# Neighbouring rows by transfers inside the chip, in place of a product with a banded matrix

## The chip, the cores and the metric

The kernel runs on one core of a Trainium2 chip. A core has a matrix engine (TensorE, PE in the profile; its weight loads are PEld), a vector engine (DVE), an activation engine (ACT), GpSimd (POOL) and SyncE (SP), which issues most of the transfers. Each engine works through its own queue of instructions in order; semaphores tie the queues together. Matrix products go from the on-chip buffer (SBUF, 128 partitions) into PSUM. Transfers run on the core's 16 DMA engines.

The metric is device time of one execution in microseconds (us). The median of several executions is given; a profiled execution beside them gives the trace.

## The reference

The input is 16 batches of 256 tokens by 256 features, all in fp32. Two layers follow each other, each with an attention and a feed-forward part:

```python
x = x + attn0(cross_attention(x, fside, ...), ...)
x = x + fp4_ffn(x @ W[cat] + b[cat], ...)
x = x + attn1(diffusion(x, zX, zY, zR), g_norm, W_qkv, W_out, pm)
x = x + mixture_of_experts(conditioned_mlp(x, ...), ...)
```

The change lies in `diffusion`, the step ahead of the second attention. `y` is the batch's x, with tokens as rows:

```python
yp_x = jnp.pad(y, ((0, 0), (0, 0), (1, 1)), mode='reflect')
lap_x = (yp_x[:, :, :-2] - 2.0 * y + yp_x[:, :, 2:]) / (dx * dx)
yp_y = jnp.pad(y, ((0, 0), (1, 1), (0, 0)), mode='reflect')
lap_y = (yp_y[:, :-2, :] - 2.0 * y + yp_y[:, 2:, :]) / (dy * dy)
du_dt = zX * lap_x + zY * lap_y + zR * y * (1.0 - y)
```

`lap_x` is the second difference along the features, `lap_y` the second difference along the tokens. At the edges the neighbour is reflected: token -1 is token 1, token 256 is token 254.

## The kernel before

The program has two parts. `woven` (L292) does everything up to the second attention for all 16 batches; `mixture` (L1034) does the conditioned MLP and the mixture of experts. The change is in the first.

A batch's x is one tile `x` of 128 partitions by 2 by 256 (token s x 128 + p lies in partition p, slot s), with five such buffers. Nine generators (the list in L310) describe the work: `stage_a` and `stage_e` the first attention, `stage_f` the first feed-forward, `stage_gate`, `stage_up` and `stage_down` the preparation of its weights, `stage_p`, `stage_g` and `stage_v` the second attention (projections, scores, values; four heads at a time, four steps n a batch). They hand single instructions to `weave` (L182), which decides while the program is built in which order each engine gets them. It keeps a planned time for each engine, each tile's last write and read (`written`, `read`), and a ring of buffers for each tag; the instruction that could start earliest goes next. Costs come from a table (L125), the hop from one engine to another is `HOP` (L126), and what SP issues counts as landed `LANDING` = 4.5 us after its issue (L127, L212). So the order of all engines is fixed in advance, from planned times; on the chip each engine then takes its instructions in this order and waits where a semaphore asks for it. `ready` (L191) computes the earliest start of an instruction: from the writes of its inputs and from the earlier writes and reads of its output's buffer.

`stage_p` (L798) loads constants once, among them the banded matrix `lap` (L801), then for each batch calls `diffuse` (L860) and four times `project4` (L897). Batch b is begun when the first feed-forward is done with it (`done["F"]`, L852), and step i = 4b + n when the values of step i - 3 have been issued (L855). `project4` loads `wq` (two buffers), `wv` (two) and `wo` (three) and multiplies them with `zT`; its last product is that of `wv`. `stage_f` issues two transfers of 1 MB of zeros to `ysort` after each batch (L612 to L614). All these loads and stores stand on SP's one queue.

`diffuse` takes a `single` PSUM bank and computes `ply` = `lap_y` there by four products with `lap` (L864 to L867; each is two records in the trace). POOL adds the left and right neighbours into `lx` (L869 to L871). Five DVE instructions make u (L872 to L876), the last of them adding zY x `ply` from PSUM. The bank is given back (L877), ACT squares u, and a few small instructions give the row's norm (L878 to L884). Four transposes on PE and two ACT copies make `zT`, tag `e_zT`, with one buffer (L885 to L892). The host builds the matrix in `tables` (L1438 to L1443).

Of the kernel before, what the change touches and what calls it, by code (L numbers as in the profile page):

```python
# [16 lines left out]
ALU = mybir.AluOpType  # L17
AX = mybir.AxisListType

P = 128  # L20
S = 256
D = 256
# [159 lines left out]
def weave(streams):  # L182

    free, written, read, rings = {}, {}, {}, {}
    turn = None
    names = lambda aps: [x.tensor.name for x in aps]

    def ready(op, engine):  # L191
        t = 0.0
        for n in names(op.ins):
            when, by = written.get(n, (0.0, engine))
            t = max(t, when + (HOP if by != engine else 0.0))
        for x in op.outs:
            n = x.tensor.name
            before = [written.get(n), read.get(n)]
            ring = rings.get(getattr(x.tensor, "tag", None), [])
            if n not in ring and ring:  # L200
                bufs = x.tensor.bufs or x.tensor.tag_meta.bufs
                if len(ring) >= bufs:
                    before += [written.get(ring[-bufs]), read.get(ring[-bufs])]
            for p in before:
                if p:
                    t = max(t, p[0] + (HOP if p[1] != engine else 0.0))
        return t

    def issue(op, choice, start):
        engine, cost, call = choice  # L210
        free[engine] = start + cost
        end = start + cost + (LANDING if engine == "SP" else 0.0)  # L212
        for n in names(op.ins):
            if end > read.get(n, (0.0, engine))[0]:
                read[n] = (end, engine)
        for x in op.outs:
            n, tag = x.tensor.name, getattr(x.tensor, "tag", None)
            written[n] = (end, engine)
            if tag is not None and n not in rings.setdefault(tag, []):
                rings[tag].append(n)  # L220
        call()

    def least(want):

        return min(want.free, key=lambda x: ready(Op([], [x], []), "PE"))


    waiting = [[s, None, None] for s in streams]
    while waiting:
        best, moved = None, False  # L230
        for rank, w in enumerate(waiting):
            while w[1] is None or (callable(w[1]) and w[1]()):
                moved = True
                try:
                    w[1], w[2] = w[0].send(w[2]), None
                except StopIteration:
                    w[0] = None
                    break
            if w[0] is None or callable(w[1]):
                continue  # L240
            if isinstance(w[1], Want):
                if not w[1].free:
                    continue
                op = Op([("PE", 0.0, None)], [least(w[1])], w[1].ins)
            else:
                op = w[1]
            for c in op.choices:
                start = max(ready(op, c[0]), free.get(c[0], 0.0))
                if c[0] == "PE" and w is not turn:
                    start += TURN  # L250
                key = (start, rank, c[1])
                if best is None or key < best[0]:
                    best = (key, w, c, start)
        waiting = [w for w in waiting if w[0] is not None]
        if best is not None:
            _, w, c, start = best
            if isinstance(w[1], Want):
                w[2] = least(w[1])
                w[1].free.remove(w[2])
            else:  # L260
                issue(w[1], c, start)
                if c[0] == "PE":
                    turn = w
            w[1] = None
        else:
            assert moved, "all streams wait"
# [12 lines left out]
def mm_(g, out, pairs, start=True, stop=True):  # L279

    last = len(pairs) - 1
    for i, (lhsT, rhs) in enumerate(pairs):
        yield g.pe.matmul(out, lhsT, rhs, start=start and i == 0, stop=stop and i == last)


def copy_(g, dst, src):

    a, v = g.act.copy(dst, src), g.dve.tensor_copy(dst, src)
    return Op(a.choices + v.choices, a.outs, a.ins)
# [23 lines left out]
def load(g, pool, name, shape, src):  # L313

    t = pool.tile(shape, F32, name=name)
    return t, g.sp.dma_start(out=t, in_=src)
# [12 lines left out]
def single(g, *ins):  # L329

    return (yield Want(g.singles, ins))
# [167 lines left out]
def row32(j, n):  # L499
    return slice(32 * j, 32 * j + n)  # L500
# [293 lines left out]
def tile_l(g, shape, name, bufs=1, tag=None):  # L794
    return g.l_.tile(shape, F32, name=name, tag=tag or name, bufs=bufs)


def stage_p(g):  # L798
    k, a = g.k, g.a
    yield lambda: g.done["A"] > 0 and g.done["W"] == 3  # L800
    g.lap, op = load(g, g.w, "lap", [P, 2, S], a["lap"])  # L801
    yield op
    g.z = []
    for n in ("condB_zX", "condB_zY", "condB_zR"):
        t, op = load(g, g.w, n, [P, g.B], a[n].unsqueeze(0).to_broadcast([P, g.B]))
        g.z.append(t)
        yield op
    g.gn, op = load(g, g.w, "g", [P, 2], a["g"])
    yield op
    g.cos1, op = load(g, g.w, "cos1", [P, S], a["cos1"])  # L810
    yield op
    g.sin1, op = load(g, g.w, "sin1", [P, S], a["sin1"])
    yield op

    g.pmo = g.w.tile([P, 2, D], F32, name="pmo")
    pmv = tile_l(g, [P, 2, 2, 2 * P], "wq", 2)
    yield g.sp.dma_start(out=pmv, in_=a["pmv"].rearrange("p c (r w) -> p c r w", r=2))
    for c in range(2):
        wo = tile_l(g, [P, 4, D], "wq", 2)
        yield g.sp.dma_start(out=wo, in_=a["w_out1"][:, 4 * c : 4 * c + 4, :])  # L820
        pmvT = tile_l(g, [P, 4, P], "f_pT", 3)
        one = yield from single(g, pmv)
        pt = one.rearrange("p (i t) -> p i t", i=4)
        for i in range(4):
            yield g.pe.transpose(pt[:, i, :], pmv[:, c, i // 2, (i % 2) * P : (i % 2 + 1) * P], g.ident)
        yield copy_(g, pmvT, pt)
        g.singles.append(one)
        one = yield from single(g, pmvT, wo)
        pm = one[:, :D]
        yield from mm_(g, pm, [(pmvT[:, i, :], wo[:, i, :]) for i in range(4)])  # L830
        yield copy_(g, g.pmo[:, c, :], pm)
        g.singles.append(one)

    g.cosq, g.sinq = g.w.tile([P, S], F32, name="cosq"), g.w.tile([P, S], F32, name="sinq")
    yield g.pool.tensor_scalar(g.cosq, g.cos1, DH1**-0.5, None, ALU.mult)
    yield g.pool.tensor_scalar(g.sinq, g.sin1, DH1**-0.5, None, ALU.mult)


    g.keys = []
    for n in range(4):  # L840
        pmk = tile_l(g, [P, 2, 4 * PM], "pmk", 2)
        yield g.sp.dma_start(out=pmk, in_=a["pmk"][:, n])
        t = g.w.tile([P, 2, 2, PM + P], F32, name=f"keys{n}")
        for j in range(4):
            rows = row32(j, 32)
            src = pmk[rows, :, j * PM : (j + 1) * PM]
            yield g.pool.tensor_copy(t[rows, :, :, 0:PM], src.unsqueeze(2).to_broadcast([32, 2, 2, PM]))
        g.keys.append(t)
    g.mhalf = g.w.tile([P, 2], F32, name="mhalf")
    yield g.pool.memset(g.mhalf, -0.5)  # L850
    for b in range(g.B):
        yield lambda b=b: g.done["F"] > b  # L852
        zT = yield from diffuse(g, b)
        for n in range(4):
            yield lambda i=4 * b + n: i < g.done["V"] + 3  # L855
            g.live[4 * b + n] = yield from project4(g, n, zT)
            g.done["P"] += 1


def diffuse(g, b):  # L860

    zx, zy, zr = (z[:, b : b + 1] for z in g.z)
    y = g.x[b]
    one = yield from single(g, y)  # L864
    ply = one.rearrange("p (s d) -> p s d", s=2)
    for st in range(2):
        yield from mm_(g, ply[:, st, :], [(g.lap[:, c, st * P : (st + 1) * P], y[:, c, :]) for c in range(2)])  # L867
    lx, u = tile_l(g, [P, 2, D], "e_lx"), tile_l(g, [P, 2, D], "e_u")
    yield g.pool.tensor_tensor(lx[:, :, 1 : D - 1], y[:, :, 0 : D - 2], y[:, :, 2:D], ALU.add)  # L869
    yield g.pool.tensor_tensor(lx[:, :, 0:1], y[:, :, 1:2], y[:, :, 1:2], ALU.add)  # L870
# [2 lines left out]
    yield g.dve.scalar_tensor_tensor(u, y, zr, u, ALU.mult, ALU.mult)  # L873
    yield g.dve.scalar_tensor_tensor(lx, y, -2.0, lx, ALU.mult, ALU.add)
    yield g.dve.scalar_tensor_tensor(u, lx, zx, u, ALU.mult, ALU.add)
    yield g.dve.scalar_tensor_tensor(u, ply, zy, u, ALU.mult, ALU.add)  # L876
    g.singles.append(one)  # L877
    ms = tile_l(g, [P, 2], "e_ms", 2)  # L878
    for st in range(2):
        yield g.act.activation(lx[:, st, :], u[:, st, :], AF.Square, accum_out=ms[:, st : st + 1])  # L880
# [5 lines left out]
    one = yield from single(g, u)  # L886
# [623 lines left out]
```

## Time and profile before

| | |
|---|---|
| time, median of 3 runs | 2941.87 us (2941.02 to 2943.33) |
| the profiled execution | 2943.53 us |
| its span, first instruction to last | 2941.8 us |
| mean granted clock of TensorE | 0.963 |
| woven part, to PE's last product before `xs` | about 1896 us |
| transfers | 265.66 MB, mean 90 GB/s |

What PE waited for longest between 200 and 1780 us of the span (total us, times, longest):

| waited for | us | times | longest |
|---|---|---|---|
| POOL `d_h` | 16.8 | 12 | 2.5 |
| POOL `c_y` | 11.0 | 9 | 3.7 |
| ACT `f_oT` | 7.4 | 15 | 0.7 |
| ACT `f_pT` | 6.5 | 15 | 1.5 |
| POOL `f_prob` | 6.4 | 3 | 4.6 |

Names are those of the program's tiles, without their numbers; `f_q<-f_t,f_t` is an instruction that writes `f_q` and reads two tiles `f_t`. Shapes are partitions by elements. Nearly all instructions of the woven part bear the line L160, as `Unit` makes them there; they are told apart by their tiles. The profile's busy time of PE sums records that overlap, so PE's price for a group of matmuls is read from the starts of the group and of the next one.

### The profile page before, as it was taken

How to read it: one execution, taken by the hardware profiler on the slowest of the kernel's cores; microseconds unless marked ns; L12 is line 12 of the kernel's file. 1: busy time of each engine (PE TensorE's matmuls, PEld its weight loads, DVE VectorE, ACT ScalarE, POOL GpSimd, SP SyncE). 2: the span in 40 equal slices, each digit the busy share in tenths (PEclk: the TensorE clock that was granted, in tenths of full speed). 3: DMA queues.
4: the chain of work that ended last, by engine and by line, in shares of the span. 5: the costliest groups of instructions: out<-in, count | busy, mean ns of one | idle time of the engine just before them, and what ended most of it. 6: DMA issues, size and time to landing. Idle time of an engine off the chain costs nothing. (4 is left out here: it accounts for less than half of the span.)

```text
span 2941.8 us, 42036 instructions
## 1 busy us (share of the span) xinstructions
PE 2768.7 (94%) x15979; PEld 2072.5 (70%) x15979; DVE 1428.6 (49%) x3073; ACT 924.0 (31%) x2416; POOL 842.2 (29%) x1023
## 2 busy tenths in 40 slices
PE   5899999999999999999999989689999999999999
PEld 3666667777777777767777767545566888888865
DVE  6566666676676676675776655413240000000023
ACT  2223333333333333423334333223321222222221
POOL 4333333433344343343343333202220000000034
PEclk7799999999899999999999999889999999999999
DMA  3122122122122132222221222231111355555523
GB/s 107 55 93 73 53 92 84 56 80 74 59 91 69 58 97 69 63 92 69 64 92 35 76 90 74 87 93 51 51 38 67 108 179 179 179 181 179 177 85 95
DMA packets 191230, 265.66 MB, mean 90 GB/s; under 512 B 34217, under 2 KB 161970, under 8 KB 181682
## 3 DMA queue, kind: packets, MB, share of 16 engines
q1 hardware_dynamic: 184882, 246.16, 26.2%
q0 software_dynamic: 6144, 16.79, 1.8%
q8 instruction: 128, 2.10, 0.3%
q14 instruction: 76, 0.62, 0.1%
HBM read 202.34 MB, written 60.56 MB: 89 GB/s over the span
## 5 line engine op out<-in xcount | busy, mean ns | idle before, releaser
L160 ACT ACTIVATE f_prob<-pair,f_stat 128x144 f32<-128x144 f32 x512 | 190.7, 377 | 270.2 <-DVE f_stat L160 258.8
L160 DVE TENSOR_TENSOR pair<-pair,mask 128x256 f32<-128x256 f32 (+1 forms) x384 | 197.8, 516 | 123.1 <-PE pair L160 83.2
L49 PE MATMUL bank<-ysT,w 128*128 128x256 f32 x1120 | 249.3, 381 | 5.7 <-ACT ysT L113 5.7
L160 PE MATMUL single<-e_zT,wq 128*128 128x256 f32 x1024 | 254.1, 392 | 0.0
L1155 POOL DMA_INDIRECT got<-osort,pos_o x64 | 62.3, 973 | 662.8 <-ACT hT L1103 608.5
L49 PE MATMUL bank<-w,ehT 128*128 128x256 f32 x1120 | 247.4, 379 | 0.0
L49 PEld LDWEIGHTS bank<-ysT,w 128*128 128x128 f32 x1120 | 211.3, 190 | 38.0 <-ACT ysT L113 9.9
L49 PEld LDWEIGHTS bank<-w,ehT 128*128 128x128 f32 x1120 | 212.8, 190 | 28.9
L160 PEld LDWEIGHTS single<-e_zT,wq 128*128 128x128 f32 x1024 | 193.4, 196 | 32.9 <-issue 2.7
L1140 ACT ACTIVATE ehT<-bank,own_b 128x256 f32<-128x256 f32 x280 | 132.5, 473 | 241.6 <-PE bank L49 241.6
L160 POOL TENSOR_SCALAR_AFFINE_SELECT b_e<-b_e 128x512 f32<-128x512 f32 x128 | 86.5, 676 | 329.9 <-ACT b_e L160 329.9
L160 PE MATMUL pair<-keys,f_q 32*128 32x144 f32 x2048 | 164.9, 300 | 0.9 <-ACT b_e L160 0.7
L160 PEld LDWEIGHTS pair<-keys,f_q 32*128 32x128 f32 x2048 | 137.2, 190 | 35.9 <-issue 28.6
L160 ACT ACTIVATE b_e<-pair 128x768 f32<-128x768 f32 x128 | 103.6, 810 | 166.4 <-PE pair L160 153.3
L160 PE MATMUL single<-wo,f_oT 128*128 128x256 f32 x512 | 129.8, 386 | 9.5 <-ACT f_oT L160 8.4
L160 POOL TENSOR_TENSOR f_q<-f_t,f_t 128x256 f32<-128x256 f32 x128 | 91.6, 734 | 160.9 <-DVE f_t L160 151.4
L160 PE MATMUL pair<-b_qkT 16*128 16x128 f32 (+1 forms) x1024 | 127.3, 373 | 11.0 <-ACT b_qkT L160 8.0
L1145 DVE COPY eo<-bank 128x512 f32<-128x512 f32 x35 | 24.2, 692 | 230.9 <-PE bank L49 230.9
L160 DVE TENSOR_REDUCE qpad<-pair 128x2 f32<-128x256 f32 (+1 forms) x256 | 131.0, 554 | 4.4
L1259 POOL DMA_INDIRECT ysort<-r_y,r_posi x64 | 62.6, 978 | 241.0 <-DMA ysort<-r_y,r_posi 97.0
L160 DVE TENSOR_TENSOR x<-x,single 128x512 f32<-128x512 f32 (+1 forms) x112 | 68.0, 607 | 128.7 <-PE single L160 128.1
L160 POOL TENSOR_TENSOR keys<-f_t,f_t 128x256 f32<-128x256 f32 x128 | 95.2, 762 | 118.8 <-DVE f_t L160 117.6
(295 smaller groups left out, 5319.7 us busy)
## 6 DMA issues: line engine op xcount, KB each, us to landing
w<-in_w SPq DMA_DIRECT2D x70, 1024.0 KB
ysort<-zero SPq DMA_DIRECT2D x32, 1024.0 KB
wq<-in_w_qk SPq DMA_DIRECT2D x128, 256.0 KB
wv<-in_w_v SPq DMA_DIRECT2D x64, 256.0 KB
wo<-in_w_out SPq DMA_DIRECT2D x64, 256.0 KB
ys<-ysort SPq DMA_DIRECT2D x35, 256.0 KB
osort<-eo SPq DMA_DIRECT2D x35, 256.0 KB
xT<-in_xT SPq DMA_DIRECT2D x16, 256.0 KB
```

Of the source, the lines that this page charges most:

```text
L49: nc.tensor.matmul(out, lhsT, rhs, start=start and i == 0, stop=stop and i == last)
L160: return Op([(self.name, self.cost(fn, outs, aps), lambda: call(*args, **kw))], outs, aps)
L1140: nc.scalar.activation(hT[:, f, :], ph, AF.Gelu_apprx_tanh, bias=b1[:, f : f + 1])
L1145: nc.vector.tensor_copy(o, po)
L1155: nc.gpsimd.indirect_dma_start(out=g, out_offset=None, in_=k.osort[:, :], in_offset=bass.IndirectOffsetOnAxis(ap=r.pos_o[:, i, t : t + 1], ...
L1259: nc.gpsimd.indirect_dma_start(out=k.ysort[:, :], out_offset=bass.IndirectOffsetOnAxis(ap=posi[:, i, t : t + 1], axis=0), in_=y, in_offset ...
```

## The change

The banded matrix and its four products go. In their place six transfers from SBUF to SBUF bring the neighbouring rows: `up` gets the row of token t - 1 and `down` that of token t + 1, each as one transfer of 127 partitions, one row of 256 from the other slot, and one reflected row. `up` is a tile of its own (tag `e_up`, one buffer), `down` uses the tag `e_zT`, whose one buffer holds `zT` later in the batch. POOL adds `down` to `up`, DVE subtracts 2y, and the last DVE instruction takes this tile where it took the PSUM bank. In `ready`, an earlier write or read of the output's buffer by SP no longer delays another instruction of SP.

```diff
@@ -202,7 +202,7 @@
                 if len(ring) >= bufs:
                     before += [written.get(ring[-bufs]), read.get(ring[-bufs])]
             for p in before:
-                if p:
+                if p and not p[1] == engine == "SP":
                     t = max(t, p[0] + (HOP if p[1] != engine else 0.0))
         return t
 
@@ -798,8 +798,6 @@
 def stage_p(g):
     k, a = g.k, g.a
     yield lambda: g.done["A"] > 0 and g.done["W"] == 3
-    g.lap, op = load(g, g.w, "lap", [P, 2, S], a["lap"])
-    yield op
     g.z = []
     for n in ("condB_zX", "condB_zY", "condB_zR"):
         t, op = load(g, g.w, n, [P, g.B], a[n].unsqueeze(0).to_broadcast([P, g.B]))
@@ -861,10 +859,17 @@
 
     zx, zy, zr = (z[:, b : b + 1] for z in g.z)
     y = g.x[b]
-    one = yield from single(g, y)
-    ply = one.rearrange("p (s d) -> p s d", s=2)
-    for st in range(2):
-        yield from mm_(g, ply[:, st, :], [(g.lap[:, c, st * P : (st + 1) * P], y[:, c, :]) for c in range(2)])
+
+    up, down = tile_l(g, [P, 2, D], "e_up"), tile_l(g, [P, 2, D], "e_zT")
+    for dst, src in (
+        (up[1:P], y[0 : P - 1]),
+        (down[0 : P - 1], y[1:P]),
+        (up[0:1, 1, :], y[P - 1 : P, 0, :]),
+        (down[P - 1 : P, 0, :], y[0:1, 1, :]),
+        (up[0:1, 0, :], y[1:2, 0, :]),
+        (down[P - 1 : P, 1, :], y[P - 2 : P - 1, 1, :]),
+    ):
+        yield g.sp.dma_start(out=dst, in_=src)
     lx, u = tile_l(g, [P, 2, D], "e_lx"), tile_l(g, [P, 2, D], "e_u")
     yield g.pool.tensor_tensor(lx[:, :, 1 : D - 1], y[:, :, 0 : D - 2], y[:, :, 2:D], ALU.add)
     yield g.pool.tensor_tensor(lx[:, :, 0:1], y[:, :, 1:2], y[:, :, 1:2], ALU.add)
@@ -873,8 +878,9 @@
     yield g.dve.scalar_tensor_tensor(u, y, zr, u, ALU.mult, ALU.mult)
     yield g.dve.scalar_tensor_tensor(lx, y, -2.0, lx, ALU.mult, ALU.add)
     yield g.dve.scalar_tensor_tensor(u, lx, zx, u, ALU.mult, ALU.add)
-    yield g.dve.scalar_tensor_tensor(u, ply, zy, u, ALU.mult, ALU.add)
-    g.singles.append(one)
+    yield g.pool.tensor_tensor(up, up, down, ALU.add)
+    yield g.dve.scalar_tensor_tensor(up, y, -2.0, up, ALU.mult, ALU.add)
+    yield g.dve.scalar_tensor_tensor(u, up, zy, u, ALU.mult, ALU.add)
     ms = tile_l(g, [P, 2], "e_ms", 2)
     for st in range(2):
         yield g.act.activation(lx[:, st, :], u[:, st, :], AF.Square, accum_out=ms[:, st : st + 1])
```

## The prediction

> **What bounds the kernel now.** I read the page's busy shares and clock first, then the busy time by stretch, then who TensorE (PE) waits for, then the instructions that the change touches.
>
> ```profile
> PE 2768.7 (94%) x15979; PEld 2072.5 (70%) x15979; DVE 1428.6 (49%) x3073; ACT 924.0 (31%) x2416; POOL 842.2 (29%) x1023
> ...
> PEclk7799999999899999999999999889999999999999
> ...
> q1 hardware_dynamic: 184882, 246.16, 26.2%
> ```
>
> PE is the full engine and its clock is nearly whole; the transfers that SP issues (q1) fill a quarter of sixteen engines. By stretch (start:end, length, then PE, PEld, DVE, ACT, POOL busy with counts, clock, DMA share, GB/s):
>
> ```profile
> 400.00:800.00 400.00, 384.08 (x2674) 290.64 (x2674) 275.43 (x554) 143.57 (x424) 151.34 (x185) 0.96 0.23 73
> 800.00:1200.00 400.00, 382.65 (x2617) 290.32 (x2614) 277.91 (x556) 143.37 (x430) 156.23 (x183) 0.98 0.25 79
> 1800.00:2000.00 200.00, 163.67 (x885) 115.26 (x884) 73.56 (x186) 56.99 (x162) 43.49 (x64) 0.90 0.29 84
> ```
>
> In the woven part (to about 1896 us) PE is 96% busy: a microsecond taken from PE is a microsecond won, and a microsecond in which PE is held up is lost, as no idle time is there to catch up in. What the change touches:
>
> ```profile
> L160 PE MATMUL single<-x,lap x128: 379/379/483, 174.0 to 1817.9; 128*128 128x256 f32 x128
> L160 POOL TENSOR_TENSOR e_lx<-x x48: 189/290/1662, 174.3 to 1816.2; 128x2 f32<-128x2 f32 x32, 128x508 f32<-128x508 f32 x16
> L160 DVE SCALAR_TENSOR_TENSOR e_lx<-x,e_lx x16: 680/684/1115, 176.4 to 1819.0; 128x512 f32<-128x512 f32 x16
> L160 DVE SCALAR_TENSOR_TENSOR e_u<-single,condB_zY,e_u x16: 750/751/752, 177.9 to 1820.5; 128x512 f32<-128x512 f32 x16
> ```
>
> Matmul records overlap, so their price is read from starts in order of time (start, length):
>
> ```profile
> 1816.41 1.89 PE L160 MATMUL single<-x,lap 128*128 128x256 f32 x8
> 1818.14 1.03 PE L160 MATMUL single<-wo,f_oT 128*128 128x256 f32 x4
> ...
> 1865.53 1.10 PE L160 MATMUL single<-ident,f_prob 128*128 128x128 f32 x8
> ...
> 1868.29 1.09 PE L160 MATMUL single<-f_pT,f_v 128*64 128x128 f32 x16
> ...
> 1881.29 1.99 PE L160 MATMUL single<-wo,f_oT 128*128 128x256 f32 x8
> 1888.34 1.97 PE L160 MATMUL single<-ident,f_prob 128*128 128x128 f32 x8 [5.05 <-POOL f_prob L160]
> 1890.23 2.18 PE L160 MATMUL single<-f_pT,f_v 128*64 128x128 f32 x16
> ```
>
> One banded product holds PE from 1816.41 to 1818.14, 1.73 us. And after a gap of 5.05 us the same two groups take 1.97 and 2.18 us where they took 1.10 and 1.09: a gap costs 2.0 us more than its length.
>
> [...] No transfer of the kernel before has 127 rows[...]: of the nine-row load `b2` (L1053) one record stands at 1913.24 us, at its issue, and nine follow at 1917.15 to 1917.57, while the 128-row `wo` issued at 1833.01 shows sixteen (1835.00 to 1836.51). [...]
>
> **The change part by part.** *Removed:* the product, 16 x 1.73 = 27.7 us of PE time on the bounding engine; the table's load (256 KB, once); one `single` bank a batch. All 27.7 us count as gain.
>
> *Added on POOL and DVE:* a 128x512 add on POOL (0.73 to 1.06 us by the other 256 and 512 wide rows) and one more `scalar_tensor_tensor` on DVE (0.68 us); the last one reads SBUF where it read PSUM (0.75, unchanged). POOL is 29% and DVE 69% busy in this part: nothing for the work itself. What counts is what these instructions wait for.
>
> *Added on SP:* six transfers a batch. SP issues one in 0.33 to 0.6 us, so about 2.6 us; SP mostly waits itself (1344 us in all for PE to release `single` tags), so the issue is free. Their duration is not. The trace's packets of 2048 bytes take 84 ns at the median, so 127 of them on one engine take 10.7 us; from the q1 line, 26.2% x 16 x 2941.8 us for 246.16 MB, the mean rate over all sizes makes it 13.0 us. Spread over sixteen it would be 0.7 us, and the landing that of `wo`, 2 to 3.5 us from issue. I take one engine and 10.7 us for each of the two big ones, in series; 13.0 and the sixteen-way spread are the ends.
>
> *When each starts.* `down` takes the buffer tag `e_zT`, so its transfer waits until PE has read the last `zT` of the batch before (the `wv` product of its fourth `project4`). `up` has a buffer of its own, and stands on SP right behind the `wo` load of that `project4`, so it starts earlier. By the order of PE's instructions in the changed program, with the prices of the trace (0.216 us a 256-wide record, 0.109 a transpose, 1.18 a group of sixteen `keys` records), `up` has 21.4 us of PE work ahead of `down` in batches 4, 6, 8, 10, 12: it is hidden. In 3, 5, 7, 9, 11 it has 14.7 us, and two 1 MB writes of zeros to `ysort` stand just ahead of it, which take about 8 us to land in the trace (issued 305.48, landed 313.6 to 315.3): `up` ends at 1 + 8 + 10.7 = 19.7, and `down` begins 4 to 5 us late.
>
> *What waits.* From that last read: 0.2 to issue, 1.0 to the first packet (as `wo` shows), 10.7, about 1.2 to the semaphore and through the four small transfers behind it: 13.1 us. Then POOL's add, 1.1, and hand-over: DVE continues at 14.6. Both engines work in order. The plan in the program puts POOL's add where a landing of 4.5 us allows it, so behind it on POOL wait the `affine_select` of `b_e` and the `keys`/`q` sums, and behind the waiting DVE instruction the mask additions, `f_stat` reductions and PSUM copies that PE needs next. In batch 4, PE's first such instruction (`a_eT`, `f`) stands 10.6 us of PE work after the last read, and DVE's copy for it comes 3.9 us after DVE continues, 18.5: a stall of about 8. In batch 5 the first is `pmo`,`f_ppT` after 6.6 us, and its copy is done at 17.3, with the 4 us lateness 21.2: a stall of 14.6. Batches 4 to 12 even: 5 x 8.1 = 40.5; 3 to 11 odd: 5 x 14.6 = 73. Batch 0 has both transfers in series from the moment x is final (0.4 + 1 + 21.4 + 0.8, add and chain 5, less 9.7 of PE work): 18. Batches 1, 2, 13, 14, 15, by the same count with 16.2, 8.6, 11.2, 8.8 and 5.8 us of work up to the `e_u` transposes: 9, 11, 10, 13, 15. Together 189.5 us.
>
> Clock after each stall: 2.0 us after 5 us idle is shown; I take 1.5 on average, 24 us. Waits that PE has already at these places and that the stall swallows: about 0.5 us a batch of the 5 us that PE idles in each, 8 us.
>
> *The planner's edit* (an SP transfer no longer counts the landing of an earlier SP transfer on the same tile) closes up the pairs of loads at the start and reorders everything. PE idles 46 us of the first 200; I bound the effect by -15 and +15 us and take 0.
>
> Sum: 189.5 + 24 - 27.7 - 8 = +178 us on the profiled execution's 2943.5 (its span is 2941.8 and 1.7 lies around it): 3121.5. The median of the runs is 2941.9, so 3120.
>
> **The rivals.** *Spread transfers, faster:* if the 127 rows go over sixteen engines, all six land within some 6 us of the trigger, the chain to `e_u` ends at about 11.5 us against 9.8 to 13.3 us of PE work, and stalls of 0 to 1 us a batch leave -27.7 + 8: 2922, at best 2914. This decides if a big transfer lands in under about 7 us. For it speaks that no trace here shows 127 rows; against it the nine-row load. Chance 0.10.
>
> *Half covered:* one engine, but PE, once free, has work that the stall has only displaced, or `up` and `down` run faster from SBUF than HBM loads did: 5 us a batch, 80 + 16 - 28 = +68, 3010. PE's 4% idle speaks against it. Chance 0.15.
>
> *Nothing covered:* 13 us each and both on the path in every batch, with the weight loads behind them on that engine late too: 26 + 3 + 5 - 11 = 23 us a batch, 368 + 32 - 28, some 3315. SP's order (`up` early) speaks against it. Chance 0.11.
>
> **How the numbers follow.** The forecast's case has 0.62, 3120, by itself 3050 to 3200; the rivals 0.10, 0.15, 0.11; 0.02 is left to a change of under 0.2% (5.9 us, about what a measurement of this kernel tells from no change), where spread transfers meet a worse order. The range 2985 to 3270 holds the forecast, the half-covered case and the near part of the last; outside lie the faster case and about 0.07 above. Faster 0.10, same 0.02, slower 0.88.
>
> **What would show it.** PE's busy time falls by about 31 us of records (128 fewer), and its waits grow. In the waits, POOL's `e_up` sum waits on a transfer, 5 to 20 us sixteen times; the clock dips below 0.9 in the woven slices; the mixture from the first `xs` transposes on lasts as long as before. If `e_up`'s add waits under 2 us, the transfers were spread and I am wrong about the sign; if it waits long and PE does not, the cover is bigger than I counted.

## The result, and the profile after

| | before | after |
|---|---|---|
| median of the runs, us | 2941.5 | 3125.0 |
| span of the profiled execution, us | 2941.8 | 3121.6 |
| ratio to before | | 1.0629 (95% interval 1.0608 to 1.0651) |
| mean granted clock of TensorE | 0.963 | 0.926 |

The forecast was 3120. The page of the changed kernel, in the lines that answer to those shown of before:

```profile
PE 2808.8 (90%) x15851; PEld 2097.8 (67%) x15851; DVE 1450.5 (46%) x3121; ACT 903.1 (29%) x2384; POOL 857.9 (27%) x1039
...
PEclk7889998899899899899998988869999999999999
...
q1 hardware_dynamic: 190882, 254.29, 25.4%
```

PE has 128 matmuls fewer and is still busy longer, at a lower clock: many of the 9s of before are 8s now over the first two thirds. The queue q1 moves 8 MB more, for a slightly smaller share of the time. By stretch (start:end, length, then PE, PEld, DVE, ACT, POOL busy with counts, clock, DMA share, GB/s), in the changed kernel:

```profile
400.00:800.00 400.00, 362.45 (x2370) 272.16 (x2368) 258.58 (x523) 124.86 (x377) 142.62 (x171) 0.92 0.23 74
800.00:1200.00 400.00, 358.48 (x2357) 270.84 (x2358) 250.10 (x503) 126.68 (x374) 142.59 (x173) 0.89 0.23 73
```

PE lost both busy share (96% to 90%) and clock (from 0.97 to about 0.9). The same view over the whole woven part and over what follows it, first of the kernel before:

```profile
0.00:1896.00 1896.00, 1759.88 (x11772) 1324.73 (x11772) 1250.03 (x2505) 659.98 (x1941) 715.88 (x879) 0.95 0.23 73
1896.00:2941.00 1045.00, 1008.78 (x4208) 747.82 (x4207) 178.55 (x568) 264.04 (x475) 126.36 (x144) 0.98 0.38 121
```

and of the changed one:

```profile
0.00:2075.60 2075.60, 1800.45 (x11644) 1350.15 (x11644) 1272.18 (x2553) 638.72 (x1909) 731.02 (x895) 0.90 0.22 71
2075.60:3121.00 1045.40, 1008.30 (x4207) 747.67 (x4207) 178.30 (x568) 264.35 (x475) 126.83 (x144) 0.98 0.38 121
```

The mixture is unchanged (1045 us, PE busy 1008). All of the loss is in the woven part, 179.6 us longer: PE is busy 40.6 us longer (1800.45 - 1759.88) and idle 139 us longer (275.2 against 136.1).

Where PE is idle begins at POOL. The instructions on the tile `e_up` (duration min/median/max in ns, then what the engine waited for ahead of them, us and times):

```profile
L160 SPq DMA_DIRECT2D e_up<-x x48: 579/772/9897, 175.9 to 1977.5; - x48
...
L160 DVE SCALAR_TENSOR_TENSOR e_up<-x,e_up x16: 692/1098/1100, 202.0 to 1988.5; 128x512 f32<-128x512 f32 x16
...
  DMA e_zT<-x: 176.7, 16
  POOL e_up L160: 129.6, 16
```

All sixteen sums wait for a transfer, 11 us on average, and DVE then waits for the sum. In order of time, batch 5 (start, length, what the engine was idle for ahead of it):

```profile
817.71 0.66 SPq L160 DMA_DIRECT2D e_zT<-x  x1
818.42 4.37 SPq L160 DMA_DIRECT2D e_up<-x  x1
...
832.33 1.26 POOL L160 TENSOR_TENSOR e_up<-e_up,e_zT 128x512 f32<-128x512 f32 x1 [13.58 <-DMA e_zT<-x]
833.63 1.10 DVE L160 SCALAR_TENSOR_TENSOR e_up<-x,e_up 128x512 f32<-128x512 f32 x1 [11.04 <-POOL e_up L160]
...
836.74 1.22 PE L160 MATMUL single<-pmo,f_ppT 128*128 128x256 f32 x2 [11.32 <-DVE f_ppT L160]
837.75 1.91 PE L160 MATMUL single<-wo,f_oT 128*128 128x256 f32 x4
```

`down` (`e_zT<-x`) is issued at 817.71, the sum begins 14.6 us later, DVE goes on, and its copy for PE comes last: PE stands 11.32 us. The `wo` group that then follows takes 1.91 us where it took 1.03. How long PE stays slow is seen in short stretches of the same view (clock third from the end):

```profile
837.00:840.00 3.00, 3.00 (x8) 2.25 (x8) 0.62 (x2) 0.24 (x2) 0.56 (x1) 0.50 0.00 0
...
849.00:852.00 3.00, 3.00 (x8) 2.37 (x8) 1.21 (x4) 0.00 (x0) 0.00 (x0) 0.50 0.00 0
852.00:855.00 3.00, 3.00 (x16) 2.22 (x16) 1.49 (x3) 0.28 (x1) 1.41 (x2) 0.85 0.00 0
```

Half speed from 837 to past 852: some 16 us of work done at half rate, 8 us lost beside the 11.32. This batch is the dearest of its kind. The 15 us from the end of the stall, in batches 5, 7 and 9, and from the end of a gap of only 1.90 us in batch 6:

```profile
836.70:851.70 15.00, 14.96 (x64) 10.57 (x65) 5.40 (x13) 2.56 (x8) 3.81 (x4) 0.50 0.22 70
1084.70:1099.70 15.00, 15.00 (x99) 11.15 (x101) 8.49 (x19) 4.00 (x13) 5.86 (x7) 0.88 0.23 72
1327.00:1342.00 15.00, 15.00 (x98) 11.15 (x100) 8.48 (x20) 4.03 (x13) 5.86 (x7) 0.88 0.22 70
949.30:964.30 15.00, 13.83 (x43) 9.90 (x44) 10.81 (x21) 3.72 (x14) 4.08 (x4) 0.57 0.63 203
```

The stalls of batches 3, 7, 9 and 11 are as long as that of batch 5 and cost about 2 us of clock each. The short gap of batch 6 costs 6 us.

### The profile page after: what moved, and what is told of

It is laid out like the page before. It is cut to its first block, busy times and chain, and to the rows that moved or that the text cites. A ratio compares the mean times of both kernels' runs of the same rounds, so it can differ in the third digit from the quotient of the medians.

```text
span 3121.6 us, 42067 instructions
## 1 busy us (share of the span) xinstructions
PE 2808.8 (90%) x15851; PEld 2097.8 (67%) x15851; DVE 1450.5 (46%) x3121; ACT 903.1 (29%) x2384; POOL 857.9 (27%) x1039
## 5 line engine op out<-in xcount | busy, mean ns | idle before, releaser
L160 PE MATMUL single<-wo,f_oT 128*128 128x256 f32 x512 | 142.9, 416 | 21.2 <-ACT f_oT L160 15.3
L160 PE MATMUL pair<-b_qS,b_qkT 17*128 17x256 f32 (+1 forms) x1024 | 127.0, 369 | 16.4 <-DVE qpad L160 10.0
L160 PEld LDWEIGHTS pair<-b_qS,b_qkT 17*128 17x128 f32 x1024 | 100.5, 204 | 51.9 <-issue 23.9
L160 PEld LDWEIGHTS single<-wo,f_oT 128*128 128x128 f32 x512 | 101.5, 208 | 43.9 <-ACT f_oT L160 18.8
```

Source lines behind the costliest of these rows:

```text
L160: return Op([(self.name, self.cost(fn, outs, aps), lambda: call(*args, **kw))], outs, aps)
```

## The experiments

Each ratio is to the kernel before on the same chip. The first four kernels ask what of the change makes the loss.

**The long transfers cut in two.** The 127 rows go as 112 and 15, which is called spread below:

```diff
-        (up[1:P], y[0 : P - 1]),
-        (down[0 : P - 1], y[1:P]),
+        (up[16:P], y[15 : P - 1]),
+        (down[0:112], y[1:113]),
+        (up[1:16], y[0:15]),
+        (down[112 : P - 1], y[113:P]),
```

> Each of the two 127-row transfers is cut into one of 112 rows and one of 15 rows; all else as in the changed kernel. Theory one-engine (a transfer of 127 rows runs on one DMA engine, two of 10.7 us each, and POOL's sum waits for the second): the pieces [...]land about 3.5 us after issue, POOL's sum waits under 2 us a batch (11 in the changed kernel), and the time falls to 2915 to 2940, near 2922. Rival order (the new order of instructions and the planner's edit cost the time, whatever the transfers do): 3080 to 3125. Rival any-wait (any transfer on the path stalls the queues): sum's wait stays over 5 us, time over 3030.

Measured: 2978.7 us, ratio 1.0117 (1.0102 to 1.0133). The waits ahead of the sum, in this kernel's `e_up` view:

```profile
  DMA e_zT<-x: 53.0, 10
  POOL e_up L160: 21.3, 7
```

Of the 183 us 146 are gone, with nothing altered in the source but the number of rows; PE takes its matmuls in the same order as in the changed kernel at 95% of the places. But none of the three ranges holds: the time lies 39 us above the first, and the sum waits 3.3 us a batch where under 2 were expected. On how many engines the pieces ran is not shown. The product's time is gone as well, and the kernel is still slower than before.

**The same, cut into 122 and 5 rows:**

> As e1, but cut into 122 rows and 5 rows[...]. Theory one-engine: the big parts take 61 x 84 ns = 5.1 us each in place of 10.7, down lands 5.5 us earlier, POOL's sum waits about 8 us in the odd batches and nothing in the even ones; between e1 and the changed kernel, 2990 to 3050. Rival order: 3080 to 3125, as in e1.

Measured: 3014.8 us, 1.0245 (1.0229 to 1.0260). Cut here, 110 of the 183 us are gone. This lies in the expected range, which took the row of packets to be half as long, 61; that is not shown. What is shown is the wait of POOL's sums for transfers: 87.3 us in all, about half of the 176.7 of the changed kernel, and 56.3 with 112 and 15 rows. That more than half of the loss goes with half of the wait would fit a landing of which a part stays covered. The three kernels together show that the loss follows this wait: 183, 73 and 37 us.

**The planner's edit alone**, on the kernel before:

```diff
-                if p:
+                if p and not p[1] == engine == "SP":
```

> The kernel before with the planner's edit in ready alone; the product with the banded matrix stays. Theory one-engine: the edit costs or gains at most 15 us, 2927 to 2957. Rival order: most of the +183 us is here, 3050 to 3125.

Measured: 2937.4 us, 0.9986 (0.9979 to 0.9992). By itself it is worth 4 us.

**The change without that edit:**

> The changed kernel without the planner's edit in ready. The three transfers into each tile then count as landing one after the other, 3 x 4.5 = 13.5 us, near the 14.4 us measured from down's issue to POOL's sum, so the plan puts other work there. Theory one-engine with a plan that counts too little: POOL's sum waits under 3 us a batch, PE's stalls go, 2920 to 2970. If the transfers hurt in another way (weight loads behind them on that engine, queue of SP blocked), the time stays over 3030.

Measured: 2978.0 us, 1.0124 (1.0107 to 1.0141). With the transfers the edit is not small at all: it costs 147 us. Without it the plan counts the three transfers into each tile one after the other, 3 x 4.5 us, and puts the sum later; with it the plan believes in 4.5 us. The time lies 8 us above the expected range, and POOL still waits (104.7 us in all, against 176.7; under 3 us a batch were expected, and most waits are of 7). PE is idle 189 us in the woven part, against 275, and works in another order. Spreading and planning each cure most of the loss, and both leave some 36 us. The next kernels look for these.

**A buffer of its own for `down`.** Two small scratch tiles are shared to make room (those lines are left out here):

```diff
-    up, down = tile_l(g, [P, 2, D], "e_up"), tile_l(g, [P, 2, D], "e_zT")
+    up, down = tile_l(g, [P, 2, D], "e_up"), tile_l(g, [P, 2, D], "e_down")
```

> The changed kernel, but `down` has a buffer of its own instead of taking turns with zT in e_zT (room for it: two of the four small scratch tiles of the down and up weights' quantization are shared). All six transfers can then be issued with `up`, 17 to 22 us ahead of the sum, and still go to one DMA engine in their long parts. If the loss is the wait between the release of e_zT and the landing: most of the 183 us goes, 2905 to 2965 us, and the sum on GpSimd waits under 40 us in all instead of 177. If the one engine's time itself were the loss (two transfers of 10.7 us in one row, 22 us), waits of 2 to 8 us in the odd batches stay and the time is 2980 to 3040. If the loss were the added elementwise work or the plan's order, 3090 to 3125.

Measured: 3068.1 us, 1.0426 (1.0380 to 1.0471). None of the three ranges holds. The second has the cause, two transfers in one row, but too small a wait. What SP issues in batch 5 of this kernel (start, length):

```profile
794.24 1.43 SPq L160 DMA_DIRECT2D e_up<-x  x1
796.11 7.91 SPq L160 DMA_DIRECT2D e_down<-x  x1
804.08 10.26 SPq L160 DMA_DIRECT2D e_up<-x  x1
814.39 1.27 SPq L160 DMA_DIRECT2D e_down<-x  x1
...
816.97 1.31 SPq L160 DMA_DIRECT2D wq<-in_w_qk  x2
```

and what the DMA engines move from 790 to 826 us, in 40 slices of 0.9 us, with the mean busy share of the sixteen in tenths:

```profile
DMA  0001799999971000000000000010000398600000
GB/s 0 0 0 27 225 312 370 372 360 364 353 246 36 14 27 25 25 25 34 25 25 23 25 25 25 25 41 26 25 27 25 94 302 285 228 23 23 23 19 6
```

After the zeros for `ysort` (370 GB/s) the rate sits at 25 GB/s from 802 to 818, about what one packet of 2048 bytes every 80 ns makes (25.6; the 80 ns are from the changed kernel), and the busy share is under a tenth in all but one of these slices (one engine of sixteen is 0.06): both long transfers on one and the same engine, one after the other. The sum begins at 824.6, 30.4 us after `up` was issued, more than the 17 to 22 us won. In batch 5 of the changed kernel the two were issued 18 us apart (800.01 and 817.71), and `up` had landed by 818.53. The buffer moves `down` from behind `zT` to behind `up`. In the even batches from 2 to 12 the sum no longer waits; in batches 5, 7, 9 and 11 it waits 11.6 to 11.8 us, and in 13 and 14 over 15.

**The same without the planner's edit:**

> The own buffer with the planner's line as it was before (a transfer waits in the plan for the landing of the one before it into the same tile). The plan then puts the sum six landings later, and the real landing lies well ahead of it. If the landing is all that counts: 2900 to 2945 us, at or below the own buffer with the edit. If a later sum costs by itself (the chain of diffuse starts the next batch's work later): 2955 to 2985, as without the edit before.

Measured: 3076.9 us, 1.0449 (1.0411 to 1.0486): neither expectation. The plan counts some 13.5 us where 25 to 31 are needed; the sum of batch 14 waits 19.2 us. All sums together wait less than with the edit (89.1 us against 134.4), and the time is no shorter; why was not found.

**Own buffer and spread transfers together:**

> The own buffer for `down` together with the 112 and 15 rows. If what stayed of the loss with spread transfers (about 36 us above the kernel before, though the product's 27.7 us are gone) is the 6.5 us from the issue of `down` to the sum: 2900 to 2935 us, faster than the kernel before. If it is the two operations more in the chain (sum on GpSimd 1.26 us, one more pass on VectorE 0.7 to 1.1 us, 16 batches) or the clock of another order: 2965 to 2985, as with spread transfers alone.

Measured: 2961.9 us, 1.0071 (1.0050 to 1.0091), with this left in the `e_up` view:

```profile
  DMA e_down<-x: 5.7, 1
```

This lies 3 us below the second expectation. PE takes its matmuls in exactly the order of the kernel with the own buffer alone, so the 106 us between these two are the spreading and nothing else. From 750 to 786 us of this kernel no stretch at 25 GB/s is left, and the one-row transfers land 2.6 (`up`) and 1.7 us (`down`) after their issue, where those of `up` took 19.7 in the stretch above. Now the transfers are hidden, one sum in sixteen waits, and the kernel is still slower than the one with the product. So landing explains at most 17 of the remaining 36 us and not the rest.

**No second difference along the tokens at all:**

> Leaves out the second difference along the tokens altogether: no product, no transfers, no sum, no two passes on VectorE. The floor for every version. If the product's 16 x 1.73 us of TensorE lie on the path: 2890 to 2918 us. If the clock or the order takes part of it back: 2918 to 2945.

Measured: 2880.5 us, 0.9783 (0.9745 to 0.9820), below both expectations. The kernel before is 62 us slower, and 57 us when the planner's edit, which this kernel has, is counted there too (2937.4). That is the price of the product, of the DVE pass that reads it and of the order of instructions that goes with them, where 28 us were counted.

**The added work without the transfers, and the transfers without the work:**

```diff
-    yield g.pool.tensor_tensor(up, up, down, ALU.add)
+    yield g.pool.tensor_tensor(up, y, y, ALU.add)
```

> Neither product nor transfers: the sum on GpSimd adds y to itself, and the two passes on VectorE follow as in the changed kernel, so the output leaves the neighbouring rows out. With an own buffer and spread transfers the sum waits only 5.7 us in all, yet 81 us stand between that kernel (2962) and the one without any of it (2880.5). If these are the price of the sum (16 x 1.3 us on GpSimd), of the passes (32 x 0.7 to 1.1 us on VectorE) and of the order they make: 2940 to 2970 us. If they are the price of the eight transfers (SP's issues, the queue): 2880 to 2900 us.

> The eight transfers into two own buffers, and nothing that reads them: no sum, no passes, no product, so the output leaves the second difference along the tokens out. If the elementwise work is the price: 2880 to 2900 us. If the transfers are: 2940 to 2965 us. In between, 2900 to 2940: each has a part of it.

Measured: 2964.0 us, 1.0077 (1.0051 to 1.0103), for the work alone; 2881.2 us, 0.9803 (0.9776 to 0.9829), for the transfers alone. Eight transfers a batch, spread and early, cost nothing measurable (2881.2 against 2880.5). This is a clean comparison: PE takes its matmuls in the same order in both kernels, the same tiles at 99.9% of 15851 places. The kernel with the work alone has the time of the own and spread version (2961.9), and its order too, again at 99.9% of the places. Between the two pairs lie 83 us. But between them the order changes as well: only 46% of the places agree. So 83 us is the price of the sum and its two passes together with the order that `weave` makes for them; no run keeps the order. Their own engine time is about 45 us (16 x 1.3 on POOL, 32 x 0.75 on DVE). The woven part, first without any of it, then with the work alone:

```profile
0.00:1837.00 1837.00, 1703.95 (x11644) 1291.81 (x11644) 1268.12 (x2506) 648.23 (x1924) 729.69 (x879) 0.95 0.24 76
0.00:1919.30 1919.30, 1766.27 (x11644) 1328.75 (x11644) 1282.67 (x2548) 641.81 (x1914) 734.77 (x895) 0.93 0.23 72
```

With the same 11644 matmuls PE is idle 20 us longer and busy 62 us longer. The clock records have it at half speed for 250 us of its busy time, against 158: this makes 46 of the 62 us, and 16 stay open. By stretch, first without any of it, then with the work alone:

```profile
400.00:800.00 400.00, 383.34 (x2740) 294.16 (x2738) 290.98 (x572) 148.85 (x452) 163.96 (x192) 0.97 0.23 73
800.00:1200.00 400.00, 383.85 (x2761) 293.80 (x2761) 298.32 (x584) 149.24 (x446) 166.64 (x194) 0.98 0.25 79
```

```profile
400.00:800.00 400.00, 376.22 (x2534) 284.83 (x2533) 276.31 (x546) 136.41 (x414) 152.74 (x181) 0.94 0.23 73
800.00:1200.00 400.00, 379.12 (x2547) 287.41 (x2547) 271.33 (x547) 134.17 (x407) 154.80 (x184) 0.95 0.23 72
```

PE's busy share falls only by 1 to 2%, and its matmul count by 8%. What happens is seen in the latter kernel at 522 to 530 us, PE's rows:

```profile
522.93 0.92 PE L160 MATMUL pair<-b_qkT 16*128 16x128 f32 x8
525.86 0.92 PE L160 MATMUL pair<-b_qS,b_qkT 17*128 17x256 f32 x8 [2.00 <-DVE qpad L160]
526.71 3.41 PE L160 MATMUL single<-e_zT,wq 128*128 128x256 f32 x8
```

and the DVE rows that end in this wait:

```profile
522.53 0.52 DVE L160 TENSOR_SCALAR q_big<-q_big 128x704 int32<-128x704 int32 x1
523.15 0.89 DVE L160 SCALAR_TENSOR_TENSOR q_y<-q_big,q_xn 128x704 f32<-128x704 f32 x1
523.96 0.69 DVE L160 TENSOR_TENSOR pair<-pair,mask 128x512 f32<-128x512 f32 x1
524.68 1.02 DVE L160 TENSOR_REDUCE qpad<-pair 128x2 f32<-128x256 f32 x2
```

DVE, 69% busy on average, works without a pause here, and comes to `qpad` too late; PE is idle for 2.00 us, and its next eight `wq` records take 3.41 us (before: 0.216 us each, 1.73 for eight). In the trace's clock records from 400 to 1600 us every one of this kernel's 19 idle stretches of 1.5 to 2.2 us is followed by half speed, about 3 us lost each. The kernel with none of the work has no stretch of this length there; it has 22 of 1.2 to 1.5 us, and half speed follows 12 of them. The added passes don't stand in the DVE rows above: those of this batch come at 546.7 and 547.4. So it is not shown that the passes themselves hold `qpad` up; the new order may.

**Less work: the terms in y gathered.** With the own buffer and the spread transfers; `g.zn` = -zr and `g.zc` are worked out once, in lines left out here:

```diff
-    yield g.dve.tensor_scalar(u, y, -1.0, 1.0, ALU.mult, ALU.add)
-    yield g.dve.scalar_tensor_tensor(u, y, zr, u, ALU.mult, ALU.mult)
-    yield g.dve.scalar_tensor_tensor(lx, y, -2.0, lx, ALU.mult, ALU.add)
+    yield g.dve.tensor_scalar(u, y, g.zn[:, b : b + 1], g.zc[:, b : b + 1], ALU.mult, ALU.add)
+    yield g.dve.tensor_tensor(u, u, y, ALU.mult)
     yield g.dve.scalar_tensor_tensor(u, lx, zx, u, ALU.mult, ALU.add)
-    yield g.pool.tensor_tensor(up, up, down, ALU.add)
-    yield g.dve.scalar_tensor_tensor(up, y, -2.0, up, ALU.mult, ALU.add)
     yield g.dve.scalar_tensor_tensor(u, up, zy, u, ALU.mult, ALU.add)
+    yield g.dve.scalar_tensor_tensor(u, down, zy, u, ALU.mult, ALU.add)
```

> A full version with the own buffer and the spread transfers, and less elementwise work: the terms in y alone are gathered (u = y(zc - zr y), with zc = zr - 2 zx - 2 zy worked out once), so that VectorE makes 5 passes a batch instead of 7 and GpSimd no sum (up and down are each added by a pass of VectorE). If the elementwise work was the rest of the loss: 2885 to 2925 us, faster than the kernel before (2942). If the transfers were: 2940 to 2965 us.

Measured: 2912.6 us, 0.9904 (0.9879 to 0.9929), in the expected range, and about 1% faster than the kernel before. Its woven part in the stretch view:

```profile
0.00:1873.40 1873.40, 1730.76 (x11644) 1294.64 (x11644) 1251.61 (x2509) 657.77 (x1940) 716.62 (x879) 0.95 0.25 79
```

The clock is back at before's 0.95, and PE's busy time is 29 us below before's 1759.88. The order is again another, so here too it is work and order together that gain 49 us over the own and spread version.

**Is that gain the transfers' or the gathering's?** The product with the same gathering and the planner's edit:

> The product of the kernel before, with the planner's edit and the terms in y gathered (zc = zr - 2 zx), so that VectorE makes 4 passes a batch instead of 5 and GpSimd works as before. It differs from the folded version with transfers (2913) only in how the neighbouring rows come in. If the gain of that version came from the fewer passes and not from the transfers: 2900 to 2918 us, as fast or faster. If the transfers, once spread and early, are worth the product's time: 2920 to 2937 us, between that version and the kernel before with the edit (2937).

Measured: 2927.4 us, 0.9952 (0.9939 to 0.9965). The interval does not touch that of the version with transfers (0.9879 to 0.9929): gathering gives about 10 us against the edit alone (2937.4), and the transfers instead of the product, with their order, some 14 more. PE's order here is that of the edit alone at 96% of the places. So this is the one place where the price of DVE work is seen with the order nearly kept: DVE's passes for u take 0.6 us a batch less by their medians, 10 us in all, and the time falls by 10 us.

## Why the prediction was right, and where it was not

The mechanism was right: one engine, a sum on POOL that waits in order, DVE and PE behind it. That the number came within 5 us is partly luck: terms that were too large met terms that were too small. Counted were 181.5 us of stalls + 24 of clock - 27.7 of product; measured are 139 + 68 - 27.7.

- *One engine, 10.7 us a transfer:* the author's estimate, with only the nine-row load to go by in the trace before; right. In batch 4 the 127 packets of `down` start from 700.85 to 712.24, 11.4 us, 119 of the 126 steps at 80 ns where a packet takes 84, so one after the other; and the semaphore shows two records, at 700.63 and 712.81. Each of the four one-row transfers issued behind it shows sixteen: fifteen within 0.8 us, before `down` lands, and the last one behind it, at 713.00, 713.19, 713.37 and 713.56. From the last packet's start to there it is 1.3 us, where about 1.2 were counted. A load issued behind them waits in the same way: in batch 5, where `down` lands at 831.30, the first `wq` has fifteen records at 827.31 to 827.92 and the sixteenth at 832.27. The two experiments with other cuts (2979 and 3015 us) agree in their times; on how many engines a piece of 112, 15, 122 or 5 rows runs was not shown.
- *Stalls, 189.5 us less 8 that they swallow:* too large; PE is idle 139 us more. Batches 0, 1, 2 and 13 to 15 came out well: their longest stalls make 81 us where 76 were counted. In the odd batches 3 to 11 PE stands 11.8 us each and not 14.6: `up` was to be 4 to 5 us late behind the zeros, but the sum comes 14.6 us after the issue of `down` in odd batches and 14.2 in even ones, so it is at most 0.4 late. The true window was 18 to 21 us where 14.7 were counted. In the even ones, 4 to 12, it stands 2.6 to 4.1 us and not 8.1: POOL itself reaches the sum later there, and waits 4.8 us where it waits 13.6 in the odd ones.
- *Clock, 24 us:* too small. PE's remaining work took 68 us more: busy 40.6 us longer with 27.7 us less to do. The clock records agree: PE works 315 us of the woven part at half speed, before 171, which makes 72 us. The step that failed is to count half speed behind the big stalls alone. There the 1.5 us of the forecast nearly held, with about 2 in batches 3, 7, 9 and 11; only batch 5 lost 8. The even batches, with gaps of 0.5 to 2.3 us, lost 5 to 10 each. For the same reason one of the forecast's signs failed: PE's busy time was to fall by about 31 us, and the page has it rise from 2768.7 to 2808.8.
- *The added work, "nothing for the work itself":* failed. DVE at 69% was taken as cover. With the order nearly kept, DVE time that fell away was won in full (the last experiment), and the sum and its passes with the order made for them cost 83 us against the floor. It is this, not the transfers, that keeps the best-hidden form of this change (2962) above the kernel before. The sum itself takes 1.26 us and not 0.73 to 1.06. In the changed kernel as it stands all this can't be separated from the clock term.
- *The product, 27.7 us:* too small, if a run without it is the measure: 57 us against the edit alone, together with the DVE pass that reads its bank and with the order. A pass less is worth about 10 us; the other 20 or so were not taken apart.
- *The planner's edit, 0 within 15 us:* right alone (4 us faster), wrong as a term that may be added. With the transfers it decides 147 us, since it is what makes the plan trust a landing of 4.5 us.
- *The rival with spread transfers* (2922, 2914 at best) fell even where the transfers are spread: 2979, and 2962 with the buffer. Its point of decision, a landing under 7 us, was met (6.1 to 7.0 us from the issue of `down` to the sum in nine of the ten batches where POOL waits for it); what it left out is the added work and the order that comes with it.

The ladder from the floor, each step a run: nothing 2881; the transfers alone 2881; the sum and passes, with another order, 2964; with hidden transfers 2962; `down` in the tag of `zT` 2979; 127 rows in one transfer 3125.

## What to carry to other kernels

Look at a transfer's packets and semaphore records before asking anything else of it: here 127 rows in one piece ran one after the other for 11.4 us and the kernel lost 183 us, cut into 112 and 15 it lost 37. And ask behind what the next one stands: an earlier start won only 57 of the 183 us while both long transfers waited in the same line. Don't cost work on a secondary engine at nothing from its average share: read the stretch in which the bounding engine waits for it, and count half-speed time behind short gaps as well as long ones. Where a plan makes the order, compare the orders of two kernels before the difference of their times is put down to the work. An edit to a planner has a price only together with what it plans.

## What the hardware showed that was not expected

- PE's clock was halved (0.50 in the clock records) after idle stretches of about 2 us, not only after long ones. From 400 to 1600 us it was after 19 of 19 stretches of 1.5 to 2.2 us with the work alone, after 18 of 19 in the own and spread version and after 3 of 5 in the kernel before. The loss did not grow with the gap: about 2 us after four of the five stalls of 11.3 us, about 6 after gaps of 1.9 us in batches 6, 8 and 10 of the changed kernel. The slow time in the clock records comes in multiples of 3.41 us: every record at 0.50 but the last one does, 25 of 26 in the kernel before and 40 of 41 in the changed one.
- SP took longer over an issue that stands behind a long transfer. In the changed kernel the one-row transfer behind `down` takes 3.6 to 4.4 us to issue in batches 1 to 14. With the own buffer the one behind both long ones takes 10.1 to 10.5, and `down` itself 7.9 to 8.3 where the zeros for `ysort` stand ahead of `up`; the one-row transfers after these take 0.6 us. What stood behind on SP's queue was issued later for it: in batch 5 with the own buffer the `wq` load was issued only at 816.97. What this costs was not measured.
